# A graph network in four layers: the loops over five turns written out as 25 turns

## The chip, the cores and the metric

The kernel runs on one core of one Trainium2 chip. Its time is the device time of one execution in microseconds. The engines have short names here, as in the profile: PE multiplies matrices, DVE and ACT work on vectors, POOL (GpSimd) issues the transfers that gather or scatter by an index, and SP issues the other transfers. Each engine executes its own list of instructions in order, and the engines wait for each other by semaphores.

## The reference

There are 12500 nodes with 32 features and 400000 edges, sorted by target. Four layers follow each other. Each gathers the source's features for every edge, makes a message of them, sums the messages by target, adds the sum to the node's features and normalises each node:

```
edge_index = jnp.stack([src, dst])
x = _layernorm(x + _L0_gnn_ref(x, edge_index, edge_weight1, edge_attr_3, edge_attr_5, L0_gnn_W), axis=-1)
x = _layernorm(x + _L1_gnn_ref(x, edge_attr_2, L1_gnn_weight, edge_index), axis=-1)
x = _layernorm(x + _L2_gnn_ref(x, edge_index, edge_attr_2, L2_gnn_g, L2_gnn_mu, L2_gnn_sigma, L2_gnn_root, L2_gnn_bias), axis=-1)
x = _layernorm(x + _L3_gnn_ref(x, edge_weight, edge_attr_3, edge_index, L3_gnn_w1, L3_gnn_b1, L3_gnn_w2, L3_gnn_b2), axis=-1)
```

Layer 0 multiplies the features by fixed coefficients and edge attributes; layer 1 weighs 16 matrices with a basis of two coordinates (and exchanges the part of source and target: it gathers by target and adds by source); layer 2 weighs three matrices with Gaussians and divides by the count of edges; layer 3 makes a matrix for every edge from a small network of its distance and applies it in the edge's own frame.

## The kernel before

A tile is 128 edges, a group 5 tiles, and a turn 25 groups (G = 25, T = 5). So 25 turns (NG = 25) make the 400000 edges. A hardware loop (`tc.For_i`) of five iterations goes over them in each layer, and each iteration has five turns written out (U = 5). Within a loop the turn's number is held in a register, and addresses that depend on it are computed by the engines.

At the end of an iteration all engines meet: each comes to the end of its list, waits for the others and for the transfers under way, the semaphores are set back, and every engine jumps to the start of the body.

**Layers 0, 2 and 3** go through `edge_pass` (L328). `begin` (L339) copies a turn's source indices, its targets relative to a base and its bases into small tiles, and calls the layer's `prepare`, which loads edge attributes and computes what the whole turn needs: `basis_rows` (L563, the basis for layer 1, done by layer 0 and stored to DRAM through PE transposes), the Gaussians (L819), the frames (L876). `turns` (L438) calls `begin` for the first turn of an iteration, and for each following turn in the middle of the turn before it. For a group, `gathered` (L349) issues five indirect gathers on POOL into a buffer `xg`, of which there are six. In layers 0 and 2 ACT copies `xg` to PSUM (`xp`, two buffers, L403). `one_hot` (L364) makes a mask of targets on DVE, the layer's `product` makes messages on DVE, and `aggregate` (L374) sums them by target in PE. `add_up` (L387) then loads the group's base, a column number, from SBUF into a register of DVE (L388) and adds the sums to the columns of an accumulator in SBUF from there on (L396). Layer 3 uses `run_ahead` (L409): the front of the next group (`tv`, `fa`, `h`) and its product with the radial weights (`pr`) are begun before the present group's `big` is reduced.

**Layer 1** has its own loop (L774) round `turn1` (L685). SP loads for each group `bas`, `rel` and `row`, and five slices `yw` of a table y_d, whose places it reads into its registers from the tile `pairs`. ACT copies `rel` to PSUM (`rel_p`, one buffer), DVE makes two masks `bm`, PE multiplies (`pe`), ACT copies the result (`msg`), PE adds up edges of the same source (`pm`), ACT copies again (`add`), and POOL adds to DRAM by five indirect scatters with accumulation.

After each layer `node_pass` (L477) adds to the features and normalises; in layers 1 and 2 the new features go to DRAM, where the next layer gathers them. Ahead of layer 0 a preamble loads indices, finds bases and ranges (`low_i`, `even`, `rel_p`, `more`), and prepares the weights (`wc`, `wr`, `b2r`). After each loop stands a fallback under `tc.If` (L457, L790) for targets further apart than a window. It isn't entered with these inputs.

The order of the instructions on each engine is set when the kernel is built: a planner goes through one straight stretch of code at a time, up to a loop or branch, and sorts the instructions by what it believes of their times, while the buffers of the pools say how far one engine may run ahead of another. A loop's body is one such stretch; what stands ahead of the loop is another.

Of the kernel before, what the change touches and what calls it, by code (L numbers as in the profile page):

```python
# [2 lines left out]

# [8 lines left out]
I32 = mybir.dt.int32  # L12
AF = mybir.ActivationFunctionType
ALU = mybir.AluOpType
AX = mybir.AxisListType
DVE = mybir.EngineType.DVE
# [7 lines left out]
G = 25  # L24
W = 64
U = 5
V = 16
EPS_LN = 1e-5

# [10 lines left out]
def kernel(  # L40
# [25 lines left out]
    nc = tc.nc  # L66
    N = x_in.shape[0]
    NG = src_t.shape[0]
    GT = G * T
# [95 lines left out]
    nid = const.tile([P, 2], F32, name="nid")  # L165
    with tc.tile_pool(name="pre1", bufs=1) as pre:
# [16 lines left out]
        nc.vector.tensor_tensor(top, top, even, ALU.subtract)  # L183
        nc.vector.tensor_scalar(top, top, int(math.log2(V)), None, op0=ALU.logical_shift_right)
        mw = pre.tile([PT, RT], F32, name="mw")
# [142 lines left out]
    def edge_pass(layer, pools, acc, prepare, product, chunks, xg_psum=False):  # L328

        io, work, ps_agg, ps_x = pools
        nch = len(chunks)
        rows = chunks[0][1] - chunks[0][0]
        nc.vector.memset(acc, 0.0)

        def begin(i):  # L339
            src = io.tile([P, GT], I32, name="src")  # L340
            nc.vector.tensor_copy(src, src_all[:, ds(i, 1), :].rearrange("p a g -> p (a g)"))
            rel = io.tile([P, G, T], F32, name="rel")
            nc.vector.tensor_copy(
                rel.rearrange("p g t -> p (g t)"), rel_all[:, ds(i, 1), :].rearrange("p a g -> p (a g)")
            )
            base = io.tile([1, G], I32, name="base")
            nc.vector.tensor_copy(base, base_i[:, ds(i * G, G)])
            return src, rel, base, prepare(i)

        def gathered(s, begun):  # L350
            xg = work.tile([P, T, F], F32, name="xg", bufs=6)
            src = begun[0]
            for t in range(T):
                nc.gpsimd.indirect_dma_start(  # L354
                    out=xg[:, t, :],
                    out_offset=None,
                    in_=x_dram[layer],
                    in_offset=bass.IndirectOffsetOnAxis(
                        ap=src[:, s * T + t : s * T + t + 1], axis=0
                    ),  # L360
                )
            return xg

        def one_hot(s, begun):  # L364
            hot = work.tile([P, T, W], F32, name="hot", bufs=4)
            nc.vector.tensor_tensor(  # L366
                hot,
                iota_w[:, None, :].to_broadcast([P, T, W]),
                begun[1][:, s, :, None].to_broadcast([P, T, W]),
                ALU.is_equal,  # L370
            )
            return hot

        def aggregate(prod, hot):  # L374
            agg = ps_agg.tile([rows, nch, W], F32, name="agg")
            for c, (a, b) in enumerate(chunks):
                for t in range(T):
                    nc.tensor.matmul(  # L378
                        agg[:, c, :],
                        prod[:, t, a:b],  # L380
                        hot[:, t, :],
                        start=(t == 0),
                        stop=(t == T - 1),
                    )
            return agg

        def add_up(s, begun, agg):  # L387
            at = nc.values_load(  # L388
                begun[2][0:1, s : s + 1],
                engines=[DVE],  # L390
                min_val=0,
                max_val=N,
                skip_runtime_bounds_check_because="a target's index or N, by the min below",
            )
            cols = acc[:, :, ds(at, W)]
            nc.vector.tensor_tensor(cols, cols, agg, ALU.add)  # L396

        def run(groups):
            for i, s, begun in groups:
                xg = gathered(s, begun)  # L400
                if xg_psum:
                    xp = ps_x.tile([P, T, F], F32, name="xp")
                    nc.scalar.copy(xp, xg)  # L403
                    xg = xp
                hot = one_hot(s, begun)
                prod = product(begun[3], i, s, xg)
                add_up(s, begun, aggregate(prod, hot))

        def run_ahead(groups):  # L409


            front, radial, multiply, reduce = product
            groups = iter(groups)

            def begin_group(g):
                if g is None:
                    return None
                i, s, begun = g
                st = front(begun[3], i, s, gathered(s, begun))
                return g, st, radial(st)  # L420

            ahead = begin_group(next(groups, None))
            last = None
            while ahead:
                (i, s, begun), st, pr = ahead
                big = multiply(st, pr)
                ahead = begin_group(next(groups, None))
                red = reduce(st, big)
                hot = one_hot(s, begun)
                if last:  # L430
                    add_up(*last)
                last = s, begun, aggregate(red, hot)
            add_up(*last)

        if isinstance(product, tuple):
            run = run_ahead

        def turns(j):  # L438
            begun = begin(j * U)
            for k in range(U):  # L440
                now = begun
                for s in range(G):
                    if s == G // 2 and k + 1 < U:
                        begun = begin(j * U + k + 1)
                    yield j * U + k, s, now

        with tc.For_i(0, NG // U, 1) as j:
            run(turns(j))


        wide = nc.values_load(
            wide_i[0:1, 0:1],
            min_val=0,
            max_val=1,
            skip_runtime_bounds_check_because="0 or 1, by the min above",
        )
        with tc.If(wide > 0):  # L457
            with tc.For_i(0, NG, 1) as i:
                src, rel, base, _ = begin(i)
                nc.vector.tensor_copy(rel_c, rel)  # L460
                nc.vector.tensor_copy(src_c, src)
                nc.vector.tensor_copy(base_c, base)
                n_win = nc.values_load(
                    wins_i[0:1, ds(i, 1)],
                    min_val=1,
                    max_val=(N - 1) // W + 1,
                    skip_runtime_bounds_check_because="a span of targets, which are below N",
                )
                with tc.For_i(0, n_win, 1):
                    nc.vector.tensor_scalar(rel_c, rel_c, float(W), None, op0=ALU.subtract)  # L470
                    nc.vector.tensor_scalar(
                        base_c, base_c, float(W), float(N), op0=ALU.add, op1=ALU.min
                    )
                    prep = prepare(i)
                    run([(i, s, (src_c, rel_c, base_c, prep)) for s in range(G)])
# [79 lines left out]
    with ExitStack() as sums_es:  # L555
      acc0 = sums_of(sums_es, 0, 124, 2)
      with ExitStack() as es:
        pools = layer_pools(es, 0)
        io, work = pools[:2]
# [77 lines left out]
    with ExitStack() as es:  # L637
        io = es.enter_context(tc.tile_pool(name="yio", bufs=2))
# [8 lines left out]
        by = 4  # L647
# [25 lines left out]
    with ExitStack() as es:  # L673
        io = es.enter_context(tc.tile_pool(name="io1", bufs=2))
# [7 lines left out]
        def load_pairs(i, to):  # L682
            nc.sync.dma_start(to, pair_d[ds(i * GT, GT)].rearrange("(a t) -> a t", a=1))
# [87 lines left out]
                        compute_op=ALU.add,  # L771
                    )

        with tc.For_i(0, NG // U, 1) as j:  # L774
            for k in range(U):
                i = j * U + k
                pairs = io.tile([1, GT], I32, name="pairs")
                load_pairs(i, pairs)
                turn1(i, pairs, nid)


        over = nc.values_load(
# [1 line left out]
            min_val=0,  # L784
            max_val=1,
            skip_runtime_bounds_check_because="0 or 1, by the min above",
# [3 lines left out]
        with tc.If(over > 0):  # L790
            with tc.For_i(0, NG, 1) as i:
# [4 lines left out]
                    min_val=1,  # L796
                    max_val=(N - 1) // V + 1,
                    skip_runtime_bounds_check_because="a span of targets, which are below N",
                )
                with tc.For_i(0, n_more, 1):  # L800
                    nc.vector.tensor_scalar(
                        pairs_c, pairs_c, float(V // 2), float(NM), op0=ALU.add, op1=ALU.min
                    )
                    nc.vector.tensor_scalar(nid_c, nid_c, float(V), None, op0=ALU.add)
                    turn1(i, pairs_c, nid_c)
# [3 lines left out]
    with ExitStack() as sums_es:  # L809
      acc2 = sums_of(sums_es, 2, 97, 1)  # L810
      with ExitStack() as es:
        pools = layer_pools(es, 2)
        io, work = pools[:2]
# [43 lines left out]
    with ExitStack() as sums_es:  # L857
      acc3 = sums_of(sums_es, 3, 80, 1)
      with ExitStack() as es:
        pools = layer_pools(es, 3, agg_bufs=1, x_bufs=0)  # L860
        io, work = pools[:2]
# [251 lines left out]
```

## Time and profile before

| what | us |
|---|---|
| median of three runs | 20443.71 (20440.81 to 20443.82) |
| the profiled execution, its own time | 20448.74 |
| its span, from the first to the last instruction | 20447.0 |
| loop of layer 0 | 116.1 to 4122.1 |
| loop of layer 1 | 4470.4 to 10583.2 |
| loop of layer 2 | 10694.6 to 14679.9 |
| loop of layer 3 | 14831.7 to 20358.0 |

| one iteration | length | PE | DVE | ACT | POOL busy |
|---|---|---|---|---|---|
| layer 0, 915.33 to 1717.51 | 802.18 | 556.96 | 290.25 | 59.05 | 602.26 |
| layer 1, 5685.00 to 6908.97 | 1223.97 | 878.14 | 538.21 | 147.89 | 972.60 |
| layer 2, 11498.40 to 12292.50 | 794.10 | 233.05 | 178.33 | 40.79 | 595.27 |
| layer 3, 15949.00 to 17051.50 | 1102.50 | 775.25 | 1007.85 | 507.55 | 606.35 |

A line of the page's groups names the kernel's line, the engine, the operation, output and inputs, and how often it ran; then the time it was busy in all, the mean of one in ns, the idle time just before, and what ended most of it. A line of the timeline has the start in us, the busy time in us, engine, line, operation, tiles and count, and in square brackets how long the engine stood idle before it and what released it. "Issue" means that the profile shows no cause for the wait. Register loads, branches and the issuing of transfers by SP are not counted as busy.

### The profile page before, as it was taken

Reading aid. Unit: us, or ns where it says so; the run is one execution under the profiler, and the core shown is the slowest. Engines: PE = TensorE matmul, PEld = TensorE weight load, DVE = VectorE, ACT = ScalarE, POOL = GpSimd, SP = SyncE. Lnnn points to the kernel's source line nnn. Section 1 sums busy time; section 2 is a strip of 40 time slices with the busy share of each in tenths; the row PEclk is TensorE's granted clock in tenths of the full one; section 3 lists DMA queues with packets and bytes.
Section 4 is the critical chain, followed back from the end, with each engine's and each line's share of the span. In section 5 each row is a group of like instructions: output and inputs, shape, how many; then the busy total and the mean of one; then the engine's idle time right before and its main releaser. Section 6 shows DMA issues by size and latency. Waiting matters only on the chain. (4 is left out here: it accounts for less than half of the span.)

```text
span 20447.0 us, 197484 instructions
## 1 busy us (share of the span) xinstructions
PE 12719.0 (62%) x51816; PEld 9979.2 (49%) x51817; DVE 10310.0 (50%) x18014; ACT 3851.0 (19%) x9168; POOL 13886.4 (68%) x12511
## 2 busy tenths in 40 slices
PE   5676676777767676776752222222467676767676
PEld 5666666656666666666652222222423333333333
DVE  3333333324444444444442222222289999999998
ACT  0000000011111111111100000000044444444443
POOL 5777777718878787887867777777555555555554
PEclk9555555555555555555555555555566666666665
DMA  1111111137767676776750000000011111111111
GB/s 39 24 25 24 23 25 24 22 104 129 129 123 129 122 129 119 132 129 122 129 106 14 15 14 14 15 13 14 10 36 31 32 31 32 31 31 32 30 31 26
DMA packets 1764667, 1156.67 MB, mean 57 GB/s; under 512 B 1103399, under 2 KB 1511663, under 8 KB 1758192
## 3 DMA queue, kind: packets, MB, share of 16 engines
q1 hardware_dynamic: 1013443, 937.43, 18.4%
q0 software_dynamic: 750000, 205.60, 11.4%
q8 instruction: 441, 7.23, 0.2%
q14 instruction: 783, 6.41, 0.1%
HBM read 1024.87 MB, written 116.94 MB: 56 GB/s over the span
## 5 line engine op out<-in xcount | busy, mean ns | idle before, releaser
L354 POOL DMA_INDIRECT xg<-x,src x6250 | 6014.2, 962 | 3691.3 <-issue 1418.3
L378 PE MATMUL agg<-hot,prod 128*124 128x64 f32 (+1 forms) x18750 | 3871.3, 399 | 3939.0 <-DVE prod L843 2822.9
L766 POOL DMA_INDIRECT sums<-add,to x3125 | 4863.0, 1556 | 1620.8 <-issue 1073.4
L378 PEld LDWEIGHTS agg<-hot,prod 128*124 128x124 f32 (+1 forms) x18750 | 3687.1, 309 | 4125.4 <-issue 4048.9
L732 PE MATMUL pe<-yw,bm 128*128 128x32 f32 x12500 | 2926.0, 403 | 1452.5 <-DVE bm L714 1349.0
L959 PE MATMUL pr<-wr,h 64*128 64x512 f32 x6250 | 3128.9, 1030 | 1104.7 <-ACT pr L954 1042.2
L354 POOL DMA_INDIRECT xg<-in_x_in,src x3125 | 3007.8, 962 | 1064.1 <-issue 810.4
L732 PEld LDWEIGHTS pe<-yw,bm 128*128 128x128 f32 x12500 | 2757.9, 329 | 1622.1 <-DVE bm L714 1489.5
L714 DVE SCALAR_TENSOR_TENSOR bm<-rel_p,nid,bas 128x640 f32<-128x640 f32 x1250 | 1090.1, 881 | 3250.8 <-ACT rel_p L711 3245.6
L959 PEld LDWEIGHTS pr<-wr,h 64*128 64x128 f32 x6250 | 1078.3, 305 | 2511.0 <-ACT pr L954 1578.8
L396 DVE TENSOR_TENSOR acc<-acc,agg 124x128 f32 (+2 forms) x1875 | 446.8, 238 | 3190.2 <-PE agg L378 3181.8
L974 DVE TENSOR_TENSOR big<-pr,fa 128x1024 f32<-128x1024 f32 x1875 | 1845.7, 1039 | 396.7 <-ACT fa L946 395.5
L954 ACT COPY pr<-b2r 128x1024 f32<-128x1024 f32 x1875 | 1594.1, 872 | 1011.8 <-DVE big L974 991.7
L985 DVE TENSOR_REDUCE red<-big 128x160 f32<-128x2560 f32 x625 | 1756.9, 2811 | 0.0
L403 ACT COPY xp<-xg 128x160 f32<-128x160 f32 x1250 | 370.0, 296 | 7272.1 <-DMA xg<-x,src 3659.9
L762 PE MATMUL pm<-msg,same 128*128 128x32 f32 x6250 | 1464.7, 403 | 272.0 <-ACT msg L740 272.0
L762 PEld LDWEIGHTS pm<-msg,same 128*128 128x128 f32 x6250 | 1380.5, 329 | 356.2 <-ACT msg L740 356.2
L843 DVE TENSOR_TENSOR prod<-gauss,xp 128x480 f32<-128x480 f32 x625 | 408.5, 654 | 1775.5 <-ACT xp L403 1749.9
L378 PEld LDWEIGHTS agg<-hot,msg 128*80 128x80 f32 x6250 | 685.2, 199 | 1260.5 <-issue 670.9
L378 PE MATMUL agg<-hot,msg 128*80 128x64 f32 x6250 | 768.9, 290 | 532.0 <-DVE acc L396 438.5
L366 DVE TENSOR_TENSOR hot<-consts,rel 128x320 f32<-128x320 f32 x1875 | 901.8, 483 | 0.0
L740 ACT COPY msg<-pe 128x160 f32<-128x160 f32 x625 | 182.5, 292 | 3734.7 <-PE pe L732 3734.7
(167 smaller groups left out, 7558.3 us busy)
## 6 DMA issues: line engine op xcount, KB each, us to landing
bas<-basis_d SPq DMA_DIRECT2D x625, 320.0 KB
rel<-rel_d SPq DMA_DIRECT2D x625, 320.0 KB
row<-in_src_n SPq DMA_DIRECT2D x625, 320.0 KB
yw<-y_d SPq DMA_DIRECT2D x3125, 32.0 KB
xg<-x,src POOLq DMA_INDIRECT x6250
dist<-in_ew_n SPq DMA_DIRECT2D x625, 96.0 KB
xg<-in_x_in,src POOLq DMA_INDIRECT x3125
sums<-add,to POOLq DMA_INDIRECT x3125
```

What stands on the lines that cost most here:

```text
L354: nc.gpsimd.indirect_dma_start(out=xg[:, t, :], out_offset=None, in_=x_dram[layer], in_offset=bass.IndirectOffsetOnAxis(ap=src[:, s * T + ...
L366: nc.vector.tensor_tensor(hot, iota_w[:, None, :].to_broadcast([P, T, W]), begun[1][:, s, :, None].to_broadcast([P, T, W]), ALU.is_equal,)
L378: nc.tensor.matmul(agg[:, c, :], prod[:, t, a:b], hot[:, t, :], start=(t == 0), stop=(t == T - 1),)
L396: nc.vector.tensor_tensor(cols, cols, agg, ALU.add)
L714: nc.vector.scalar_tensor_tensor(bm[:, h], rel_p, ids[:, h : h + 1], bas, op0=ALU.is_equal, op1=ALU.mult)
L732: nc.tensor.matmul(pe[:, t, :], bm[:, h, t, :], yw[:, t, h * F : (h + 1) * F], start=(h == 0), stop=(h == 1),)
L762: nc.tensor.matmul(pm[:, t, :], same[:, t, :], msg[:, t, :], start=True, stop=True)
L766: nc.gpsimd.indirect_dma_start(out=sums[t], out_offset=bass.IndirectOffsetOnAxis(ap=to[:, t : t + 1], axis=0), in_=add[:, t, :], in_offset ...
L954: nc.scalar.copy(pr[:, : b - a, :], b2r.rearrange("p o u j -> p (o u j)")[:, None, :].to_broadcast([P, b - a, 512]),)
L959: nc.tensor.matmul(pr[:, k, :], h[64 * k : 64 * k + 64, a // 2, :], wr[64 * k : 64 * k + 64].rearrange("h o u j -> h (o u j)"), start=Fals ...
L974: nc.vector.tensor_tensor(big[:, a * 4 : b * 4], pr[:, : b - a, :].rearrange("p t (o u j) -> p (t o) u j", u=8, j=16), fa[:, a * 4 : b * 4 ...
L985: nc.vector.tensor_reduce(red.rearrange("p t o u -> p (t o) u"), big, AX.X, ALU.add)
```

## The change

The four hardware loops of five iterations are gone: all 25 turns of each layer stand in the program one after the other. `turns` gets the first turn and the number of turns, so that only the layer's first `begin` has no turn ahead of it. The turn's number is a constant. Since a stretch of code is now a whole layer (and the layer's preamble with it), the planner could place register loads far ahead of the additions that use them; a list `adds` holds the additions, and `issue_after` makes each load follow the addition of the group before. The fallbacks keep their loops.

```diff
+WHOLE = (0, 1, 2, 3,)
...
-        def add_up(s, begun, agg):
-            at = nc.values_load(
-                begun[2][0:1, s : s + 1],
-                engines=[DVE],
-                ...
-            )
+        def add_up(s, begun, agg, adds):
+
+            with tc.issue_after(adds[-1].ins) if adds else nullcontext():
+                at = nc.values_load(
+                    begun[2][0:1, s : s + 1],
+                    engines=[DVE],
+                    ...
+                )
             cols = acc[:, :, ds(at, W)]
-            nc.vector.tensor_tensor(cols, cols, agg, ALU.add)
+            adds.append(nc.vector.tensor_tensor(cols, cols, agg, ALU.add))
...
-        def turns(j):
-            begun = begin(j * U)
-            for k in range(U):
+        def turns(i0, n):
+            begun = begin(i0)
+            for k in range(n):
                 now = begun
                 for s in range(G):
-                    if s == G // 2 and k + 1 < U:
-                        begun = begin(j * U + k + 1)
-                    yield j * U + k, s, now
-
-        with tc.For_i(0, NG // U, 1) as j:
-            run(turns(j))
+                    if s == G // 2 and k + 1 < n:
+                        begun = begin(i0 + k + 1)
+                    yield i0 + k, s, now
+
+        if layer in WHOLE:
+            run(turns(0, NG))
+        else:
+            with tc.For_i(0, NG // U, 1) as j:
+                run(turns(j * U, U))
...
-        with tc.For_i(0, NG // U, 1) as j:
-            for k in range(U):
-                i = j * U + k
-                pairs = io.tile([1, GT], I32, name="pairs")
-                load_pairs(i, pairs)
-                turn1(i, pairs, nid)
+        for i in range(NG):
+            pairs = io.tile([1, GT], I32, name="pairs")
+            load_pairs(i, pairs)
+            turn1(i, pairs, nid)
```

## The prediction

> **What bounds the kernel now.** The page comes first, for the engine and the groups.
>
> ```profile
> PE 12719.0 (62%) x51816; PEld 9979.2 (49%) x51817; DVE 10310.0 (50%) x18014; ACT 3851.0 (19%) x9168; POOL 13886.4 (68%) x12511
> ...
> L354 POOL DMA_INDIRECT xg<-x,src x6250 | 6014.2, 962 | 3691.3 <-issue 1418.3
> ...
> L766 POOL DMA_INDIRECT sums<-add,to x3125 | 4863.0, 1556 | 1620.8 <-issue 1073.4
> ```
>
> No engine is full, and each layer has its own limit, so the timeline by layer comes next. POOL at the end of a loop iteration of layer 0:
>
> ```profile
> 907.00 0.94 POOL L354 DMA_INDIRECT xg<-in_x_in,src  x1 [0.31 <-issue]
> 917.75 0.97 POOL L354 DMA_INDIRECT xg<-in_x_in,src  x1 [9.81 <-DVE base L347]
> ...
> 921.53 1.73 POOL L354 DMA_INDIRECT xg<-in_x_in,src  x1 [0.30 <-issue]
> ```
>
> Inside an iteration a gather starts every 1.249 us (0.94 busy, 0.30 issue), in layer 2 as well: both are paced by POOL, 5 x 1.249 = 6.245 us a group. At the iteration's end POOL stands for 9.81 us, until the others have drained and the next `src` is copied. Layer 1, same place, then inside:
>
> ```profile
> 5698.82 1.56 POOL L766 DMA_INDIRECT sums<-add,to  x1 [0.30 <-issue]
> 5726.27 1.55 POOL L766 DMA_INDIRECT sums<-add,to  x1 [25.89 <-DMA rel<-rel_d]
> ```
>
> ```profile
> 5001.16 4.05 PE L732 MATMUL pe<-yw,bm 128*128 128x32 f32 x18 [0.22 <-DVE bm L714]
> ...
> 5005.30 0.29 ACT L740 COPY msg<-pe 128x160 f32<-128x160 f32 x1 [5.97 <-PE pe L732]
> 5005.64 2.34 PE L762 MATMUL pm<-msg,same 128*128 128x32 f32 x10 [0.44 <-ACT msg L740]
> ...
> 5008.21 0.70 ACT L711 COPY rel_p<-rel 128x640 f32<-128x640 f32 x1
> ...
> 5008.95 0.88 DVE L714 SCALAR_TENSOR_TENSOR bm<-rel_p,nid,bas 128x640 f32<-128x640 f32 x1 [5.20 <-ACT rel_p L711]
> ```
>
> A ring bm, pe, msg, pm, add, rel_p closes every 9.59 us (bm at 4999.36, then 5008.95); POOL's five scatters need 5 x 1.86 = 9.3. Layer 3 is DVE at its loop end:
>
> ```profile
> 15948.94 0.22 DVE L396 TENSOR_TENSOR acc<-acc,agg 80x64 f32 x1 [1.75 <-PE agg L378]
> 15951.67 0.23 DVE L341 COPY src<-src_all 128x125 int32 x1 [2.52 <-PEq L447]
> 15955.67 0.55 DVE L881 TENSOR_TENSOR sq<-sh 128x375 f32<-128x375 f32 x1 [1.75 <-DMA sh<-in_sh_t]
> ...
> 15972.76 0.30 DVE L933 TENSOR_TENSOR tv<-xg,fr 128x120 f32<-128x120 f32 x1 [4.69 <-DMA xg<-x,src]
> ```
>
> Its window of one iteration has DVE busy 1007.85 of 1102.50 us. The waits here are drain, refill and a cold prepare.
>
> **What the Trainium skill says.** "Runtime: NRT & Kernel Launch", section Instruction fetch mechanics: fetch is sequential and streamed in blocks, [...]and a taken branch out of the window stalls. The trace agrees on the streaming:
>
> ```profile
> q8 instruction: 441, 7.23, 0.2%
> q14 instruction: 783, 6.41, 0.1%
> ```
>
> That is 13.6 MB; at the page's 16 KiB for 256 instructions (64 B each) 197484 executed ones make an estimated 12.6 MB. So every iteration is already fetched anew, and straight code fetches no more. "SBUF — State Buffer", section Who interferes with whom, has a DVE operation with two SBUF inputs hinder GpSimd's reads, but says tensor_tensor didn't stall descriptor writing. Here it does: the gather at 921.53 took 1.73 beside `d` (L567), others up to 2.94 beside `basis` (L577). These belong to each turn and stay.
>
> **The change, part by part.** I read the starts of the first gather (scatter) of each turn off POOL's timeline, and compare an iteration with five inner turns.
>
> Layer 0: iterations 802.1, 802.7, 800.8, mean 801.9; inner turns 157.65, 158.64, 158.91, mean 158.4, so 5 x 158.4 = 792.0. A boundary costs 9.9, and four go: 39.5.
> Layer 1: iteration 1224.9; inner turns 239.71, 240.16, 239.53, 239.85, so 1199.1. 25.9 each: 103.5.
> Layer 2: iterations 795.6, 796.6, 796.3, mean 796.2; inner 158.80, 158.83, 156.03, 156.04, so 787.1. 9.1 each: 36.4.
> Layer 3: 1102.4, 1103.8, 1102.5, mean 1102.9; inner 218.45, so 1092.3. 10.6 each: 42. POOL's own gap of 61 us there is mostly its lead being lost, not time of DVE.
>
> Together 221.4. The last drain of each layer stays. In the built order the steady groups are the same as before on DVE and ACT in layers 0, 1 and 3, and SP's dynamic address steps go (SP waits 172.5 us in 63 groups of layer 1, 2.7 each, so this is worth nothing).
>
> Start of layer 0: no loop stands ahead of it now, so DVE copies `src` once src_all is in, not at 116.6. In the DMA records the 12800-byte packets of the next load, d_i, begin at 8.3 us, by when some 800 packets of 2000 bytes (src_all has 1.6 MB) have passed; with the receipt I take 11 us. POOL's order then has 40 gathers, 50 us, ahead of the iota `pid` (L197), for which DVE waits: pid comes near 65 (11 + 50, and 4 for gathers lengthened by DVE) instead of 42.7. DVE's preamble before:
>
> ```profile
> 42.90 0.15 DVE L198 TENSOR_SCALAR pid<-pid 128x1 int32<-128x1 int32 x1
> ...
> 56.79 3.49 DVE L173 TENSOR_REDUCE even<-t_i 125x25 int32<-125x3200 int32 x1 [13.49 <-DMA t_i<-in_dst_n]
> ...
> 83.54 3.40 DVE L191 TENSOR_REDUCE more<-mw_row 1x25 f32<-1x3125 f32 x1 [15.51 <-DMA mw_row<-mw_d]
> ...
> 92.61 21.00 DVE L337 MEMSET acc<- 124x25128 f32 x1 [5.30 <-DMA b2s<-in_l_b]
> ```
>
> After pid DVE has two reduces (7.0), small ones (0.6), `d` (1.2), one product (0.8) and rel_p (3.5), to 78-79; before, rel_p ended at 67.5. The memset began 25.1 after rel_p's end, since rel_p is first stored: now it starts at 104 and ends at 125; the weight and bias sums (7) and two additions stand ahead of the third product, done at 135. Meanwhile POOL has made ten groups (six xg buffers, and four copies to xp that the first two products let go), to 76, and stands until the fifth copy. Its group 10 starts at 135; before, at 117.1 + 10 x 6.245 + 1 = 180.6. Afterwards DVE and PE need some 5.7 us a group (4.37 for PE's twenty passes, product and addition around them), under POOL's 6.245, so the lead is kept. Worth 46; bounds 0 (DVE later by another 46) and 58 (DVE as early as before).
>
> The register load: L388 stood directly ahead of the addition in most groups, and does now, behind the preceding addition. It runs while DVE works (0.30 us, sequencer only): nothing. Layer 2 had some loads ahead; now none. DVE is busy 178 of 794 us there, which covers them. If it were bare in layer 3: 625 x 0.30 = 188.
>
> The order also puts parts of layer 2's prepare between the layernorm steps ahead of the store of x, where DVE is alone: six operations of 0.93, one behind ACT's root: 5 lost.
>
> Sum: 221.4 + 46 - 5 = 262.4. Profiled execution 20448.7 - 262.4 = 20186.3; the median of the runs lies 5.0 lower: 20181 us.
>
> **The rivals.** (a) The start gains nothing, since pid and the in-order preamble hold DVE: 20181 + 46 = 20227. For it: pid really is queued behind 40 gathers, and DVE's `basis` waits for ACT in mid-preamble. Against: DVE idled 13.5 and 15.5 us there.
> (b) The load is bare: 20181 + 188 = 20369. For: it now waits for an addition. Against: that addition ended a group earlier, and the order on the queue is as it was.
> (c) Slower: fetching straight code. 441 + 783 blocks are fetched; if each made its engine, on the layer's limit, stand 0.214 us more, 262 us, the gain is gone. At 0.4 us: 490, that is 20671. Against: the pace of 1.249 inside 625 unbranched gathers shows no such stand.
> (d) More: layer 2 settles at its 156.0 us turns (24 x 1.4 = 34), and the start brings 58: 20181 - 34 - 12 = 20135.
> That the change doesn't do what it says is out: no branch is left in the four passes except the fallback.
>
> **How the numbers follow.** Forecast 0.72, whose own range is 20158 to 20210; (a) 0.10, (b) 0.04, (c) 0.05, (d) 0.09. A measurement tells 0.2% (41 us) from none. All but (c) and a part of (b)'s tail are faster: 0.93; same 0.02; slower 0.05. The range 20130 to 20242 takes in (a) and (d), and leaves out (b), (c) and the tails of the rest.
>
> **What would show it.** POOL's starts: a constant 1.249 through layers 0 and 2, no gap near 10, only the begin's long gathers; layer 1 with 239.8 in every turn and no gap of 26; layer 3 with 218.45; first gather near 11, a stand of POOL from about 76 to 135; pid near 65. I'm wrong if the turns change: a ring other than 9.59 in layer 1, or additions of layer 3, away from a turn's prepare, further apart than the 8.1 and 9.0 us of now.

## The result and the profile after

The changed kernel takes 20169.9 us (median; 20169.6 to 20175.8), the kernel before 20443.0 (20440.8 to 20443.8): a ratio of 0.9865, 95% interval 0.9853 to 0.9878, or 273 us less. The forecast was 20181 us, 262 less. The profiled execution went from a span of 20447.0 to 20168.0 us, 279.0 less; the one before lay 5.7 us above its median (20448.74 against 20443.0), the one after on it.

The page of the kernel after: the engines, POOL's two groups, and the two queues that fetch instructions (packets and MB).

```profile
PE 12755.3 (63%) x51816; PEld 9989.1 (50%) x51817; DVE 10300.1 (51%) x18014; ACT 3844.3 (19%) x9161; POOL 13889.9 (69%) x12511
...
q8 instruction: 425, 6.96, 0.2%
q14 instruction: 670, 5.48, 0.1%
...
L355 POOL DMA_INDIRECT xg<-x,src x6250 | 6025.0, 964 | 3587.2 <-issue 1538.1
...
L774 POOL DMA_INDIRECT sums<-add,to x3125 | 4854.7, 1554 | 1520.3 <-issue 1082.7
```

The work is the same; POOL's idle time ahead of its gathers and scatters has shrunk (3691 to 3587, 1621 to 1520), and slightly less code is fetched than before, not more. Now the places of the old boundaries. POOL in layer 0, where turn 5 begins (start, duration, idle time before it and what ended it):

```profile
868.53 0.94 POOL L355 DMA_INDIRECT xg<-in_x_in,src  x1 [0.30 <-DMA xg<-in_x_in,src]
869.77 0.94 POOL L355 DMA_INDIRECT xg<-in_x_in,src  x1 [0.30 <-issue]
871.02 0.94 POOL L355 DMA_INDIRECT xg<-in_x_in,src  x1 [0.30 <-issue]
```

Where POOL stood for 9.81 us, the pace of 1.25 us goes on. The same place in layer 1:

```profile
5615.04 1.55 POOL L774 DMA_INDIRECT sums<-add,to  x1 [0.30 <-issue]
5617.63 1.55 POOL L774 DMA_INDIRECT sums<-add,to  x1 [1.03 <-issue]
```

The gap of 25.89 us is 1.03. The ring of layer 1 is what it was: below, two steps of `bm` lie 9.59 us apart (5616.81 and 5626.40). The additions of layer 3, last, stay 8.1 and 9.0 us apart.

```profile
5616.81 0.88 DVE L722 SCALAR_TENSOR_TENSOR bm<-rel_p,nid,bas 128x640 f32<-128x640 f32 x1
...
5621.88 0.29 ACT L748 COPY msg<-pe 128x160 f32<-128x160 f32 x1 [5.97 <-PE pe L740]
...
5624.80 0.70 ACT L719 COPY rel_p<-rel 128x640 f32<-128x640 f32 x1
...
5626.40 0.88 DVE L722 SCALAR_TENSOR_TENSOR bm<-rel_p,nid,bas 128x640 f32<-128x640 f32 x1
...
15499.83 0.20 DVE L399 TENSOR_TENSOR acc<-acc,agg 80x64 f32 x1
15508.80 0.20 DVE L399 TENSOR_TENSOR acc<-acc,agg 80x64 f32 x1
15516.92 0.20 DVE L399 TENSOR_TENSOR acc<-acc,agg 80x64 f32 x1
```

The start of layer 0, all of the kernel after: POOL's lines with a stand and `pid`, then DVE, then ACT, then PE:

```profile
10.00 1.10 POOL L355 DMA_INDIRECT xg<-in_x_in,src  x1 [8.14 <-DVE src L342]
...
62.58 0.15 POOL L198 IOTA pid<- 128x1 int32 x1
80.36 0.95 POOL L355 DMA_INDIRECT xg<-in_x_in,src  x1 [17.63 <-ACT xp L407]
...
143.57 0.94 POOL L355 DMA_INDIRECT xg<-in_x_in,src  x1 [50.38 <-ACT xp L407]
```

```profile
62.77 0.15 DVE L199 TENSOR_SCALAR pid<-pid 128x1 int32<-128x1 int32 x1 [18.02 <-POOL pid L198]
...
96.66 2.24 DVE L585 TENSOR_TENSOR basis<-d 128x2000 f32<-128x2000 f32 x1 [14.28 <-PE pb L600]
...
100.05 3.39 DVE L192 TENSOR_REDUCE more<-mw_row 1x25 f32<-1x3125 f32 x1
...
109.12 21.00 DVE L338 MEMSET acc<- 124x25128 f32 x1 [5.30 <-DMA w2s<-in_l_w]
...
132.44 0.21 DVE L277 COPY we<-pw 124x48 f32<-124x48 f32 x1
...
137.13 0.29 DVE L399 TENSOR_TENSOR acc<-acc,agg 124x128 f32 x1 [0.81 <-PE agg L379]
...
141.26 0.29 DVE L399 TENSOR_TENSOR acc<-acc,agg 124x128 f32 x1 [3.55 <-PE agg L379]
141.47 0.81 DVE L621 TENSOR_TENSOR prod<-sh,xp 128x640 f32<-128x640 f32 x1
```

```profile
94.38 0.59 ACT L604 COPY bs<-pb 128x512 f32<-128x512 f32 x1 [9.73 <-DMA basis_d<-bs]
```

```profile
106.77 1.03 PE L269 MATMUL pw<-wm,rows 8*124 8x48 f32 x4 [0.95 <-DMA wm<-in_w]
...
132.70 8.53 PE L379 MATMUL agg<-hot,prod 128*124 128x64 f32 x40 [17.10 <-DVE we L277]
```

The first gather starts at 10.0 us instead of 117.1, but the gain is what is left at group 10, whose first gather starts at 143.57 instead of 180.65: 37 us.

From the first and last gather (scatter) of each layer on POOL's timeline, the whole difference falls into these parts:

| part, us | before | after | less | forecast |
|---|---|---|---|---|
| layer 0, start to group 10 | 180.65 | 143.57 | 37.1 | 46 |
| layer 0, from there to its last gather | 3934.1 | 3894.8 | 39.3 | 39.5 |
| layer 0's last gather to layer 1's first scatter | 387.6 | 380.3 | 7.3 | 0 |
| layer 1 | 6096.2 | 5994.7 | 101.5 | 103.5 |
| layer 1 to layer 2 | 111.0 | 111.1 | -0.1 | -5 |
| layer 2 | 3965.6 | 3916.0 | 49.6 | 36.4 |
| layer 2 to layer 3 | 175.4 | 172.8 | 2.6 | 0 |
| layer 3 | 5453.5 | 5412.3 | 41.2 | 42 |
| after layer 3's last gather | 142.9 | 142.5 | 0.4 | 0 |

### The profile page after: what moved, and what is told of

The parts are those of the page before. It is cut to its first block, busy times and chain, and to the rows that moved or that the text cites. A ratio compares the mean times of both kernels' runs of the same rounds, so it can differ in the third digit from the quotient of the medians.

```text
span 20168.0 us, 188789 instructions
## 1 busy us (share of the span) xinstructions
PE 12755.3 (63%) x51816; PEld 9989.1 (50%) x51817; DVE 10300.1 (51%) x18014; ACT 3844.3 (19%) x9161; POOL 13889.9 (69%) x12511
## 5 line engine op out<-in xcount | busy, mean ns | idle before, releaser
L965 PE MATMUL pr<-wr,h 64*128 64x512 f32 x6250 | 3170.8, 1043 | 1059.6 <-ACT pr L960 1059.5
```

The costliest lines, as they stand in the source:

```text
L965: nc.tensor.matmul(pr[:, k, :], h[64 * k : 64 * k + 64, a // 2, :], wr[64 * k : 64 * k + 64].rearrange("h o u j -> h (o u j)"), start=Fals ...
```

## The experiments

The theory: a loop boundary costs a drain, a refill and a cold prepare, each by itself; straight code and the register load cost nothing; DVE's preamble bounds the start. The rivals: the cost of a boundary is code fetched anew; the load is bare; another engine or queue bounds the start. The first four kernels ran on a chip where the kernel before takes 20443 us, as in the result; the other eight ran on two chips where it takes 22519 (second chip) and 22380 us (third chip). So each is compared on its own chip only.

**Layer 1 alone, and the three edge passes alone.**

```diff
-        with tc.For_i(0, NG // U, 1) as j:
-            for k in range(U):
-                i = j * U + k
+        for i in range(NG):
```

This, on the kernel before, is the first kernel. The second is the kernel after without it.

> Layer 1 alone written out, the three edge passes looped as before. If a boundary of layer 1 costs its 25.9 us wherever the other layers stand: 4 x 25.9 = 103.5 less, and some 7 us less between layer 0's last gather and layer 1's first scatter, so about 20443 - 110 = 20333 us, with turns of 239.8. If straight code is fetched at a cost that the saved boundary hides, the turns are longer than 239.8 and the gain is smaller. If the gain of the whole change comes out of layers together, this one is below 90.

Measured: 20332.1 us against 20443.5, 111.4 less. Layer 1 takes 5994.2 us, with turns of 239.8.

> Layers 0, 2 and 3 written out, layer 1 looped as before. If the layers' gains add: 76 (layer 0, boundaries and start) + 50 (layer 2) + 3 + 41 (layer 3) = 170 less, about 20273 us, and layer 1 with its five iterations of 1224.9. If layer 1's loop stands in the way of something else, the sum of this gain and of layer 1's alone misses 279 us by more than 10.

Measured: 20281.4 us, 162.1 less. The two gains make 273.5; the whole change brought 273.1. They add, and layer 1 with its loop keeps its 6093 us. The 8 us missing against the expected 170 lie in layer 2 (3923.6 instead of 3916.0 us, the same code, see below). The two kernels also divide the row of the table that shows no change. Between layers 1 and 2 the first has 103.8 us, the second 116.2, before had 111.0: leaving layer 1's loop was worth 7.2, and layer 2's prepare between the layernorm steps costs 5.2. In the whole change both are there and nearly hide each other; together they would leave 109.0 us, and 111.1 was measured, so these two gains add only to within 2 us.

**25 turns in a loop of one iteration.**

```diff
-U = 5
+U = 25
-WHOLE = (0, 1, 2, 3,)
+WHOLE = ()
```

and layer 1's loop as before.

> All 25 turns written out, but inside a loop of one iteration in each layer: no boundary is left, the entry to the loop stays, and so do the addresses that hang on the loop's register. If boundaries give 221 to 235 us and the absent loop entry ahead of layer 0 and layer 1 the other 44: first gather near 117 us as before, and 20443 - 235 = about 20208 us. If the layer-0 start is not due to the loop's entry: first gather near 10 us and about 20170 us. If addresses worked out in registers had cost time: above 20230 us.

Measured: 20231.3 us, 212.2 less: a little over the expected end, at the edge named for costly addresses. By layer: layer 0 from its first to its last gather 33.9 less, layer 1 102.2, layer 2 35.3, layer 3 43.0; together 214.4 against 221.4 forecast for the boundaries. The first gather starts at 116.4 and group 10 at 181.1, as before the change: the early start is due to there being no loop to enter. Layers 1 and 3 take no longer than in the straight version, although their addresses hang on a register; so the addresses cost nothing there. Against the straight version, layer 2 lacks 14 us, which the records of its gathers account for (below).

**One turn per iteration.**

```diff
-U = 5
+U = 1
```

on the kernel before.

> One turn per iteration: 24 boundaries in each layer in place of 4. If a boundary costs by itself what it was read to (9.9, 25.9, 9.1, 10.6 us in layers 0 to 3, 55.5 together): 20 x 55.5 = 1110 us more, about 21553 us. If what it costs is code fetched anew, which goes with the instructions and not with the number of boundaries: about as before, 20443 us. If a boundary costs less where only one turn's lead is lost: layers 0, 2 and 3 give less than 9 us each, in between.

Measured: 21358.3 us, 914.8 more. The page of this kernel:

```profile
span 21353.8 us, 202188 instructions
...
q14 instruction: 345, 2.83, 0.0%
q8 instruction: 37, 0.61, 0.0%
```

and POOL at one of its boundaries in layer 0:

```profile
284.44 0.95 POOL L354 DMA_INDIRECT xg<-in_x_in,src  x1 [9.44 <-DVE base L347]
```

The two fetching queues within layer 0, before (130 to 4110 us), then with one turn per iteration (130 to 4290 us), where q14 fetches nothing:

```profile
q8 instruction: 104, 1.70, 0.2%
q14 instruction: 102, 0.84, 0.1%
```

```profile
q8 instruction: 3, 0.05, 0.0%
```

A boundary of layer 0 is still a stand of some 9 us until `base` is copied. Twenty more of them cost 183.1 us in layer 0, 422.9 in layer 1, 107.6 in layer 2 and 195.3 in layer 3: 9.2, 21.1, 5.4 and 9.8 each instead of 9.9, 25.9, 9.1 and 10.6. Layer 2's are cheaper here for two reasons that the records show: POOL stands for some 7.1 us at each instead of 8.6 to 10.2, and its gathers are 18.5 us shorter in sum (2957.2 against 2975.7), since no prepare stands in the midst of an iteration. Why the stands of layers 1 and 2 are shorter here was not tested. The cost goes with the number of boundaries. The fetch cannot be its cause: only 3.4 MB of code are fetched, against 13.6 before, for more instructions executed; in layer 0 next to nothing is fetched, and each of its boundaries costs 9.2 us all the same.

**Layer 2's gathers.** How long POOL is busy with layer 2's gathers, before, after, in the loop of one iteration, and with the three edge passes alone written out (from layer 2's first gather to its last; length, then POOL busy):

```profile
10709.58:14675.19 3965.61, 2975.68 (x3125) 0.50 0.09 14
```

```profile
10524.43:14440.43 3916.00, 2964.01 (x3125) 0.50 0.09 14
```

```profile
10570.28:14500.61 3930.33, 2978.52 (x3125) 0.50 0.08 14
```

```profile
10630.18:14553.80 3923.62, 2971.78 (x3125) 1.00 0.08 14
```

Where the gathers take about as long as before (2978.5), the layer gains 35.3, about the 36.4 of the forecast. After the change they are 11.7 us shorter in sum than before, and the layer gains 14 more. Among the three kernels without a boundary in layer 2, the length follows the gathers one for one: 6.7 us less for 6.7 less, then 7.6 less for 7.8 less. A gather takes 0.94 us as a rule; before, 63 of layer 2's took over 1 us, 55 of them beside one of the three products `d` of prepare, and in the loop of one iteration 61 of 62; after the change 34 of only 35. To take these products away:

```diff
-            d = io.tile([P, GT, 3, 2], F32, name="d")
...
-            nc.scalar.activation(gauss, gauss, AF.Exp, scale=-0.5)
+            nc.scalar.activation(gauss, u[:, :, 0:1].to_broadcast([P, GT, 3]), AF.Exp, scale=-0.5)
```

> The whole change, with layer 2's prepare left without its three products d, their sum and so the right gauss (the exponential of u stands in for it). If the gathers of layer 2 that take longer than 0.94 us are those beside these products: every turn is 156.05 us, 24 x 0.55 = 13 us less, about 20157 us. If they come from one_hot, additions or the loads of src: turns stay at 156.6 on average and the time at 20170.

> Again the whole change with layer 2's prepare left without its three products and their sum (the exponential of u stands in for gauss). If the long gathers of layer 2 are those beside these products: all turns 156.05 us, 13 us less than the whole change. If not: turns of 156.6 on average and no gain.

> The kernel before, looped, with the same products of layer 2's prepare left out. If layer 2's gain of 50 us is four boundaries of 9.1 and some 13 of fewer collisions: here no collision is left, inner turns are all 156.05, and layer 2 is about 3966 - 26 to 40 = 3926 to 3940 us, so that the layer without loop and products (about 3902) is 24 to 38 us shorter. If the 13 us are part of what a boundary costs: the difference of the two stays near 50.

Measured: on the second chip 21910.0 us, without the whole change beside it; on the third, in one run each, 21794.5 against 21808.7 for the whole change (14 less) and, looped, 22359.3 against 22379.8 (20 less). That the size fits proves little: on these chips layer 2's turns take 174 to 192 us and POOL does not pace them, so the expected 156.05 could not appear, and looped and straight differ by 116 us in layer 2 without any product. So the cause of the 14 us rests on the records of the first chip, where length and gathers go together, and no run there took the products away; why fewer gathers meet a product after the change is open. One thing can be read: between layers 1 and 2, 106.3 us instead of 110.2, so without the products 3.9 of prepare's 5 us in the layernorm go.

**The register load, written twice.**

```diff
             with tc.issue_after(adds[-1].ins) if adds else nullcontext():
+                at = nc.values_load(
+                    begun[2][0:1, s : s + 1],
+                    engines=[DVE],
...
+                )
                 at = nc.values_load(
```

> The whole change, with each group's register loaded twice (1875 loads more, 0.30 us each on DVE's sequencer). If the load is covered by the addition and other work of DVE: no change, 20170 us within 10, and the additions of layer 3 stay 8.1 and 9.0 us apart. If it is bare wherever DVE is the limit, layer 3 alone grows by 625 x 0.30 = 188: 20358 us.

Measured: 22002.7 us on the second chip. Layer 3 takes 5439.7 us, and 5439.4, 5437.4 and 5439.6 in the three other kernels there. But this run doesn't test the load: its trace has 1875 loads, as before, all of the second one (L398). Of the first one (L391), whose register nothing uses, only a semaphore instruction of 21 ns is left:

```profile
L391 DVEq EVENT_SEMAPHORE  x1889: 21/21/50, 63.9 to 21915.3; - x189
L398 DVEq TENSOR_LOAD <-base x1875: 298/304/554, 136.8 to 21915.4; - x188
```

What settles the question is the trace of the kernel after. A load takes 0.30 us of the sequencer there, in layer 3 191 us in all; DVE's own work runs on beside it, and during only 0.9 of these 191 us was DVE idle. Before, it was 1.2 us. Layer 3's turns are 218.45 us before and after, where a bare load would have added 7.5 to each. So the load is covered. What the ordering of the loads, a part of the change, is worth by itself no run shows.

**The start: pid ahead of the gathers.**

```diff
+    pid = const.tile([P, 1], I32, name="pid")
+    nc.gpsimd.iota(pid, pattern=[[0, 1]], base=0, channel_multiplier=1)
+    nc.vector.tensor_scalar(pid, pid, 4, None, op0=ALU.logical_shift_right)
     psc = ctx.enter_context(tc.tile_pool(name="psc", bufs=1, space=PSUM))
...
-        nc.gpsimd.iota(pid, pattern=[[0, 1]], base=0, channel_multiplier=1)
```

> The whole change, with the iota pid and its shift ahead of all gathers instead of behind 40 of them. DVE then stands until t_i is in (about 57 us, as before the change) and not until 62.8. If that wait is what made DVE's preamble late, even starts at 57 instead of 64.5, acc's memset and the third product come 7 to 8 us earlier, and group 10's first gather starts near 136 instead of 143.6: about 20162 us. If DVE's later waits (for the transposes of basis, for the load of mw_row) set the start, nothing is gained: 20170 us, group 10 at 143 to 144.

Measured on the second chip: 21944.2 us. DVE of this kernel:

```profile
61.72 3.49 DVE L177 TENSOR_REDUCE even<-t_i 125x25 int32<-125x3200 int32 x1 [16.18 <-DMA t_i<-in_dst_n]
```

DVE now waits for `t_i` itself, which lands 5 us later than before the change. Group 10 starts at 141.03; the kernels with the late iota on that chip have it at 144.33 and 144.65. So pid's place was worth some 3.4 us, not 7 to 8.

**The start: layer 1's tables moved into layer 0's node pass.** The block that makes pid, even, top, rel_p and more becomes a generator of ten steps:

```diff
-    with tc.tile_pool(name="pre1", bufs=1) as pre:
+    def pairs_of(pre):
...
+        yield
...
                 if layer != 2:
                     nc.vector.tensor_tensor(zb, xb, pt, ALU.add)
+                    next(beside, None)
...
+      with tc.tile_pool(name="pre1", bufs=1) as pre:
-      node_pass(0, acc0, [wc0[:124, 0, :], wc0[:124, 1, :]])
+        node_pass(0, acc0, [wc0[:124, 0, :], wc0[:124, 1, :]], pairs_of(pre))
```

> The whole change, with the tables of layer 1 (pid, even, top, rel_p, more) worked out between the additions of layer 0's node pass, where DVE stands 8.7 us at a time, instead of ahead of layer 0. If the stand of POOL from 93 to 143.6 us is DVE's preamble: acc's memset starts near 45, the third product comes at 75 to 80, group 10 starts near 85, 55 to 60 us earlier, and at most 5 are given back in the node pass: about 20115 us. If the SP queue (weights, sh, u, the stores of basis) sets the start, group 10 stays later than 120 and the gain is under 25 us.

> The whole change once more, as the measure for the runs beside it, since chips differ. On a chip like the first: 20170 us, group 10 of layer 0 at 143.6 us, turns of 158.4 in layer 0 and 156.0 to 157.4 in layer 2. On a chip like that of the runs with the register loaded twice: about 22000 us, with turns near 200 and 184 in these layers and 239.8 and 218.5 in layers 1 and 3.

> Again the whole change with the tables of layer 1 worked out between the additions of layer 0's node pass. On a chip where layer 0 is paced by POOL, and if DVE's preamble is what POOL stands for: group 10 starts near 85 us, 55 to 60 earlier, some 2 us are given back between layers 0 and 1, and the time is about 20113 us. If the lead that POOL wins at the start is lost again later in layer 0: no more than 20 us, 20150.

Measured: 21908.3 us on the second chip; on the third, with the whole change beside it, 21761.3 (21755.1 to 21764.7) against 21808.7 (21806.1 to 21810.3): 47.4 less, and the fastest kernel there (0.9725 of before, 0.9708 to 0.9741; the whole change has 0.9746, 0.973 to 0.9762). POOL of the whole change on this chip, then POOL and DVE of the version with the tables moved:

```profile
144.14 0.94 POOL L355 DMA_INDIRECT xg<-in_x_in,src  x1 [50.44 <-ACT xp L407]
```

```profile
80.89 2.63 POOL L367 DMA_INDIRECT xg<-in_x_in,src  x1 [18.55 <-ACT xp L419]
96.97 0.94 POOL L367 DMA_INDIRECT xg<-in_x_in,src  x1 [2.21 <-ACT xp L419]
```

```profile
49.80 21.00 DVE L350 MEMSET acc<- 124x25128 f32 x1 [5.18 <-issue]
...
78.49 0.82 DVE L634 TENSOR_TENSOR prod<-sh,xp 128x640 f32<-128x640 f32 x1
```

The stand of 50 us is 2, group 10 starts 47.2 us earlier, and all of it reaches the end (416.2 us to layer 1 instead of 416.5: the moved work is hidden). So the tables, which stood in DVE's list ahead of the memset, bounded the start. The version moves DVE's work on them and their transfers in SP's queue together, so it doesn't tell which of the two cost more. The 85 us expected missed by 12: the first product now stands behind the memset and the weight sums, at 78.49 instead of 72.55 in the kernel after, so group 8 starts no earlier than it did (80.89). This version was not run on a chip like that of the result.

## Why the prediction was right

The time lies 11 us below the forecast and inside its range, and the mechanism is the one named. That the total came so close is in part luck: terms of some 28 us were missing, others were some 12 too large, and another 5.7 went because the profiled execution before lay above its median. By its steps:

- **Boundaries.** Layers 0, 1 and 3 gave 39.3, 101.5 and 41.2 us for 39.5, 103.5 and 42. The single-iteration loop and the one-turn loop confirm that these are boundaries, each with its own price. How a price divides into drain, refill and cold prepare no run separates.
- **Layer 2.** "9.1 each: 36.4" holds for the boundaries (35.3 in the loop of one iteration). The term that was mis-sized is the turn: 787.1 for five was taken as fixed (of the gathers lengthened beside DVE's products: "These belong to each turn and stay"), and it came down to 783. Thus 49.6, part of the way to rival (d), "layer 2 settles at its 156.0 us turns".
- **Start.** "Worth 46": 37.1. pid came at 62.8 (forecast 65), and POOL stood, as said, after ten groups, at 93 rather than 76, since group 8 already waited 17.6 us for DVE's products. The third product came 6.5 us late, and the lines above show two waits that the forecast didn't have. DVE stood 14.28 us for the second `basis`, since ACT's copy `bs`, which frees PE's `pb`, waited 9.73 us for the stores of the first basis; so the memset began at 109.1, not 104. And PE's first products `agg`, whose `hot` and `prod` had been there since 81.3, started at 132.70, when DVE had made the second copy `we`, which stands behind the memset; so two additions waited for PE. The products `pw`, which `we` copies, were done by 107.8. Why `agg` waits for a copy that it doesn't read isn't shown; by the kernel, the PSUM pool of `pw` is closed before that of `agg` is opened, so `agg` may take its place. Rival (a), no gain at the start, is out: the version with a loop of one iteration shows what the start is without it.
- **"The last drain of each layer stays."** This step was wrong for two layers: leaving a loop gave 7.3 us at the end of layer 0 (7.4 with layer 1 still looped) and 5 to 7 at the end of layer 1 (111.0 to 103.8 us by one pair of kernels, 116.2 to 111.1 by the other). It was not in the sum. The 2.6 us at the end of layer 2 are not shown to come from there: the kernels with loops of one iteration and of one turn leave a loop too, and have 172.3 and 173.0 us instead of 175.4.
- **Layer 2's prepare in the layernorm**, "5 lost": 5.2 by the version with layer 1 looped; with layer 1 written out it is 7.3 (103.8 us with layer 2 looped, 111.1 in the whole change).
- **Register load**, nothing: the traces show it covered, and layer 3's turns did not grow. Rival (b) is out.
- **Straight code**, rival (c), is out: turns of 239.8 and 218.5 as before, less code fetched (12.4 MB for 13.6). But the reason given, that every iteration is already fetched anew, holds for bodies of five turns only: with bodies of one turn three quarters of these bytes are not fetched again. The Trainium skill ("Runtime: NRT & Kernel Launch", Instruction fetch mechanics) gives a stall only where a branch leaves the current window of two blocks. The traces agree that a short body isn't fetched again (three packets in all of layer 0), but PE's body there is longer than two blocks of 16 KiB: some 1060 instructions a turn, an estimated 68 KB at the 64 B that follow from that section. So on PE more than that stays. The forecast's "441 + 783 blocks" are packets, those of q14 of some 8 KB each (6.41 MB in 783).

In sum, some 14 us from leaving the loops of layers 0 and 1 and 13 from layer 2's turns were missing, and 9 of the start were too many; the rest are single microseconds.

## What to carry to other kernels

Read what a loop boundary costs as the length of an iteration less that of its inner turns, layer by layer; summed over the boundaries it foretold the gain within a few per cent. Work that comes forward when a loop is gone meets the preamble in the queues of the other engines: follow the first products of the new start through DVE's and PE's order, and move what only a later stage needs into a stage where the engine stands. Measure the variant and its reference on one chip, and look in the trace whether an instruction that was added for an experiment is there at all.

## What the runs showed of the hardware

The three chips differ by 10% on the same kernel before (20443, 22519 and 22380 us), nearly all of it in layers 0, 2 and 3, and with them the gain: on the third chip the change brings 571 us. DVE's waits there, of the whole change (waited for: us in total, times, longest):

```profile
DVE acc L399 <- remote: 4871.5, 469, 26.1
```

"Remote" means that a semaphore ended the wait and the profile does not tell who set it. In the six traces with 20443 us for the kernel before, no wait of DVE is of this kind. On the third chip it falls nearly all on one instruction, the addition whose address comes from a register, and on layers 0 and 2. In the looped kernel (without layer 2's products) on that chip, after a boundary of layer 3, DVE and then POOL:

```profile
17775.41 0.69 DVE L959 TENSOR_TENSOR big<-pr,fa 128x512 f32<-128x512 f32 x1 [3.31 <-remote]
17801.59 0.22 DVE L396 TENSOR_TENSOR acc<-acc,agg 80x64 f32 x1 [25.49 <-remote]
```

```profile
17795.96 0.94 POOL L354 DMA_INDIRECT xg<-x,src  x1 [0.30 <-issue]
17809.83 0.94 POOL L354 DMA_INDIRECT xg<-x,src  x1 [12.93 <-ACT pr L939]
```

PE had ended the sum at 17775.7, the register was there at 17776.4, and the addition began only 4.7 us after POOL, which had issued gathers without a pause since 17740.5, stopped. The other three boundaries of layer 3 look the same: the addition stands for 25.5 to 26.9 us and begins 4.7 to 5.0 us after POOL's burst. An iteration of layer 3 is 1133.2 us there, 41 more than five turns, instead of 10.6. Without boundaries these four stands, 104 us in sum, are gone; they make up most of the 129 us by which layer 3 gained more on that chip (170 us) than on the first (41). That POOL's burst holds the addition up is argued from these four places. Against it stands that at the start of layer 3 such an addition, after 21.9 us, began 0.7 us before POOL's burst was over (the whole change on the third chip). What the addition waits for, and why one chip does not know the wait, no run here tells.
